# Feed-forward weights through a rounded DRAM copy and SP's queue, with new tables of order, in a four-layer transformer kernel

## The chip, the cores and the metric

The kernel runs on one NeuronCore of a Trainium2 chip. The metric is the device time of one execution in microseconds; 3622.65 is the median of three runs of the kernel before (3621.72 to 3628.54).

The engines go by short names: PE is TensorE, DVE is VectorE, ACT is ScalarE, POOL is GpSimd, SP is SyncE, which issues transfers and computes nothing. Every engine carries out its own instructions in a written order and waits on semaphores for the others.

## The reference

The input x is 8 batches of 512 tokens of width 256, in fp32. Four residual layers follow one another, each behind a layer norm:

```python
x = x + attn_a(layernorm(x)); x = x + ffn(layernorm(x))
x = x + attn_b(layernorm(x)); x = x + ffn(layernorm(x))     # the same ffn weights both times

# attn_a: 16 heads of 64; the "sequence" of the softmax is the 64 components of one head of one token
scores[q, k] = Q[q] * K[k] / 8, masked to k <= q;  w = softmax_k(scores);  out[q] = sum_k w[q, k] * V[k]
# attn_b: ordinary causal attention over the 512 tokens, 16 heads of 16
# ffn: ternary weights (-1, 0, 1) with scales by row
h = silu(x @ w1.T * s1) * (x @ w2.T * s2)
h = gelu(h @ h1.T * s_h1);  h = gelu(h @ h2.T * s_h2);  out = h @ w3.T * s3
```

So attn_a is elementwise work: for each token and head a triangle of 64 x 64 products, exponentials and weighted sums. It falls to POOL, DVE and ACT. The feed-forward layers and attn_b fall mostly to PE.

## The kernel before

**Attention A.** A unit of work is one block of 128 tokens (i of 4) and one group of four heads (g of 4): 16 units for each batch, 128 in all. The lower triangles of a unit are cut into squares of width n = 32, 16, 8, 4, 2 and 1, kept in four tiles: unit 0 and unit 2 of `units` (32-wide squares), unit 1 (16-wide), and unit 3 (8, 4, 2 and 1). A tile goes through these steps:

- `scores` multiplies queries by keys (POOL for units 0 to 2, DVE for unit 3; L855),
- `exps` is the exponential on ACT (L878),
- `weigh` multiplies by the values on DVE (L890),
- `halve` adds one half of a 128 x 4096 tile to the other by an accumulating 1 MB transfer that POOL issues (L897),
- for unit 2, `fold` adds two halves on POOL (L905),
- the sums over the columns follow: unit 0 by 16 accumulating transposes on PE (`sums32`, L918), a copy, a turn back and an add on DVE (L1000); the others by DVE reduces (`gather`, L1047) and adds on POOL (`adds`, L1063).

DVE then inverts the denominators (`invert`, L1069), POOL multiplies (`divide`, L1075), PE turns the group over and projects it out (L1085, L1101, L535).

**The order.** A unit has a period of 12 slots. The table `G["order"]` gives every step a slot relative to the unit's start and, by its place in the table, a rank within the slot; `first` is the table of batch 0. Units overlap, since the slots run from -120 to 36. A manual schedule keeps the written order on PE, DVE, ACT and POOL.

**The rest.** A generator (`after_a`) yields the feed-forward layer, attn_b and the second feed-forward layer of each batch piece by piece. The main loop interleaves it with attention A of the following batch: `G["pace"]` prices the pieces, and `G["total"]` is what is spent on them over the 16 units of a batch. Attention A of batch 0 runs alone at the start, and the rest of the last batch alone at the end.

**Feed-forward weights.** PE multiplies them in a rounded type, F32R, while DRAM holds fp32. A pass reads 11 tiles of 128 x 2048 (1 MB): two for the gates (L1293), eight hidden ones (L1365) and w3 (L1398). There are two passes for each batch, so 16 passes and 176 loads. The pool `hwp` has three buffers. `Weights.ahead` issues the load after the next one; POOL issues it, as a transfer that converts on the way. The weights of attn_b (`wbqk`, `wbvp`) come in the same sequence from SP. In the last pass `fits` loads the unrounded tiles once more by SP (L1250) and compares them with the rounded ones on DVE.

SP also issues attention A's weights (L730, L732, L738), x and the stores of the output.

Of the kernel before, what the change touches and what calls it, by code (L numbers as in the profile page):

```python
# [16 lines left out]
P = 128  # L17
# [28 lines left out]
 'half': [0, 0, 0, 0, 1, 1],  # L46
 'order': [[8, 'scores', 2, 1, 2], [10, 'exps', 2], [22, 'small_squares'], [20, 'add16'], [-120, 'load'],
           [-26, 'normalise'], [6, 'exps', 1], [13, 'sums32', 0], [23, 'adds', 3], [32, 'turn_group'],
           [22, 'keep_sums', 2], [16, 'keep16'], [9, 'weigh', 1], [-1, 'scores', 0, 0, 2], [11, 'fold', 0],
           [12, 'turn16'], [6, 'halve', 0], [11, 'scores', 3, 0, 1], [-30, 'ahead'], [14, 'sums16'],  # L50
           [22, 'add32', 2], [12, 'weigh', 2], [21, 'turn_sums', 2], [34, 'project_out'],
           [4, 'scores', 1, 1, 2], [-8, 'project'], [10, 'halve', 1], [36, 'new_x'], [25, 'divide'],
           [13, 'weigh', 3], [7, 'scores', 2, 0, 2], [15, 'turn_sums', 0], [17, 'fold', 2], [32, 'keep_att'],
           [-5, 'keep_qk'], [12, 'halve', 2], [13, 'keep_sums', 0], [18, 'add32', 0], [18, 'gather', 3],
           [-22, 'turn_x'], [24, 'invert'], [13, 'gather', 1], [16, 'adds', 1], [20, 'sums32', 2],
           [12, 'exps', 3], [4, 'weigh', 0], [3, 'exps', 0], [1, 'scores', 1, 0, 2], [-22, 'keep_x'],
           [0, 'scores', 0, 1, 2]],
 'first': {'sum': ['pe16', 'pe16'],
           'p16': 2,
           'sum16': 'dve',  # L60
           'order': [[21, 'small_squares'], [23, 'adds', 3], [21, 'sums32', 2], [-23, 'turn_x'],
                     [29, 'divide'], [0, 'scores', 0, 1, 2], [4, 'scores', 1, 0, 2], [15, 'turn16'],
                     [26, 'invert'], [19, 'add32', 0], [6, 'scores', 2, 0, 2], [6, 'halve', 0],
                     [-1, 'scores', 0, 0, 2], [-27, 'normalise'], [9, 'fold', 0], [7, 'exps', 1],
                     [10, 'exps', 2], [20, 'gather', 3], [15, 'turn_sums', 0], [4, 'weigh', 0],
                     [23, 'turn_sums', 2], [15, 'weigh', 3], [-120, 'load'], [-30, 'ahead'], [16, 'keep16'],
                     [10, 'scores', 3, 0, 1], [-21, 'keep_x'], [17, 'adds', 1], [19, 'sums16'],
                     [23, 'add32', 2], [8, 'weigh', 1], [10, 'halve', 1], [36, 'new_x'],
                     [4, 'scores', 1, 1, 2], [13, 'weigh', 2], [-5, 'keep_qk'], [6, 'scores', 2, 1, 2],
                     [14, 'exps', 3], [31, 'turn_group'], [21, 'add16'], [21, 'keep_sums', 2],  # L70
                     [15, 'gather', 1], [32, 'keep_att'], [13, 'fold', 2], [14, 'sums32', 0],
                     [14, 'keep_sums', 0], [-8, 'project'], [34, 'project_out'], [13, 'halve', 2],
                     [2, 'exps', 0]],
           'on': ['adds0']},
 'sum16': 'dve',
 'lo': 'psum',
 'pace': {'gate': 1.8, 'attn': 0.65, 'wait': 1.354, 'w3': 1.05, 'out': 0.95, 'turn': 0.997},
 'total': 304.842,
 'eps': 'dve',
# [7 lines left out]
       'attn': 72,  # L87
       'proj': 21}}

# [243 lines left out]
def fast_path(ctx: ExitStack, tc: tile.TileContext, k, t, flag):  # L333
# [216 lines left out]
    def bank_half(j):  # L550
        return bank[:, j, :]
# [86 lines left out]
    JB = 8  # L638

    def kind(b, n_u):  # L640
        c = G["first"] if b == 0 and "first" in G else G
        return c["sum"][n_u // 2] if n_u in (0, 2) else c.get("sum16", "dve")

    def reds(b):
        return (G["first"] if b == 0 and "first" in G else G).get("red", [])

    def on(b):
        return (G["first"] if b == 0 and "first" in G else G).get("on", [])

    def p16(b):  # L650
        return (G["first"] if b == 0 and "first" in G else G)["p16"]

# [3 lines left out]
    def pieces(w, n, off, nsq, cols, b, n_u, parts):  # L656
# [6 lines left out]

        if n < 16:
            e, ev = (
# [42 lines left out]
    class AttentionA:  # L708
# [32 lines left out]
        def slot(self, t):  # L741

            now = []
            for lo, hi, order in TABLES:
                for place, (slot, what, args) in enumerate(order):
                    late = 8 if what in ("normalise", "turn_x", "keep_x") and t - slot in (12, 20) else 0
                    n, r = divmod(t - slot - late, 12)
                    if r == 0 and lo <= n < hi and (late == 0 or t - slot == 20):
                        now.append((place / len(order), what, self.todo[n] + args))
            for _, what, args in sorted(now, key=lambda p: p[0]):  # L750
                getattr(self, what)(*args)
# [177 lines left out]
        def sums16(self, b, i, g):  # L929

            if kind(b, 1) == "dve": return
            assert (b, i, g, 1, "h") in self.seen
            w = self.live.pop((b, i, g, 1)).rearrange("p (j r) -> p j r", r=2 * P)
            self.take(1, 0, 1)
            for r in range(2):
                for j in range(8):
                    nc.tensor.matmul(
                        bank_half(1)[:, r * P : (r + 1) * P], w[:, j, r * P : (r + 1) * P], ident,
                        start=(j == 0 and r == 0), stop=(j == 7), is_transpose=True, skip_group_check=True,
                    )  # L940
            assert "fwd" not in self.live
            self.live["fwd"] = (b, i, g, 1)

        def keep16(self, b, i, g):

            if kind(b, 1) == "dve": return
            assert self.live.pop("fwd") == (b, i, g, 1)
            self.live["sums16"] = ap_.tile([P, 2 * P], F32, tag="red128", name="sums16", bufs=3)
            nc.scalar.copy(self.live["sums16"], bank_half(1))
            self.free(1, 0, 1)  # L950

        def turn16(self, b, i, g):

            if kind(b, 1) == "dve": return
            assert "back" not in self.live
            self.live["back"] = (b, i, g, 1)
            s16 = self.live.pop("sums16")
            self.take(1, 0, 1)
            for r in range(2):
                nc.tensor.transpose(bank_half(1)[:, r * P : (r + 1) * P], s16[:, r * P : (r + 1) * P], ident)  # L960

        def add16(self, b, i, g):

            if kind(b, 1) == "dve": return
# [3 lines left out]
            nc.vector.tensor_tensor(  # L968
                rows, rows, bank_half(1).rearrange("p (a x i) -> p a x i", a=2, i=16), ALU.add
            )  # L970
            assert (b, i, g, 0, "w") in self.seen
            self.free(1, 0, 1)
            self.done[b, i, g] += 1
# [40 lines left out]
        def small_squares(self, b, i, g):  # L1014
# [4 lines left out]
            for n, off, nsq, cols in squares(units[NU - 1]):  # L1019
                if n <= 2 and n not in reds(b):  # L1020
# [3 lines left out]
                    self.add_rows(b, i, g, n, cols, both[..., 0], "small")  # L1024
            if (b, i, g, NU - 1, "r") in self.seen: self.live.pop((b, i, g, NU - 1))

        def gather(self, b, i, g, n_u):
# [4 lines left out]
            w = self.live[b, i, g, n_u]  # L1032
            if n_u < NU - 1 or (b, i, g, n_u, "s") in self.seen: self.live.pop((b, i, g, n_u))
            self.sums[b, i, g, n_u] = []
            here = 0
            for n, off, nsq, cols in sorted(squares(units[n_u]), key=lambda u: u[0] in reds(b)):
                if n in reds(b):
                    assert all((b, i, g, k, what) in self.seen for k in range(NU) for what in "pew")
# [87 lines left out]
    def flush():  # L1126
        fns = pending[:]
        pending.clear()
        for fn in fns:
            fn()  # L1130

    class Weights:

# [3 lines left out]
        def __init__(self):  # L1137
            def ffn():
                for i in range(MC // 4):
                    yield "gate", F32R, nc.gpsimd, t.w12p[i]  # L1140
                for layer in range(2):
                    for i in range(MC // 2):
                        yield "hidden", F32R, nc.gpsimd, t.h12[layer, i]
                yield "w3", F32R, nc.gpsimd, t.w3p

            def all_of_them():
                for b in range(NB):
                    yield from ffn()
                    yield "wbqk", F32, nc.sync, wbqk_d
                    yield "wbvp", F32, nc.sync, wbvp_d  # L1150
                    yield from ffn()

            self.n, self.todo, self.loaded = 0, all_of_them(), []
            for _ in range(2):
                self.ahead()

        def ahead(self):
            what = next(self.todo, None)
            if what is not None:
                name, dtype, eng, src = what  # L1160
                w = hwp.tile([P, HB], dtype, tag="hw", name=f"{name}_{self.n}")[:, : src.shape[-1]]
                eng.dma_start(w, src)
                self.loaded.append(w)
                self.n += 1
# [594 lines left out]
```

## Time and profile before

| What | Value |
|---|---|
| median of three runs | 3622.65 us |
| profiled execution, its own time | 3620.43 us |
| its span | 3618.6 us |
| mean granted clock of PE | 0.916 |
| busy, share of the span | PE 84%, DVE 86%, ACT 69%, POOL 82% |
| software queue (POOL's transfers) | 587.24 MB, 71.1% of 16 DMA engines |
| hardware queue (SP's and ACT's transfers) | 75.02 MB, 6.0% |
| halvings, issue to landing | 384 of 1 MB, median 7.6 us |
| feed-forward weights, issue to landing | 128 + 32 + 16 of 1 MB, median 6.0 to 6.7 us |

A row of a group of instructions reads: line, engine, operation, output<-input, shapes, count | busy us, mean ns of one | idle us of the engine just before them, and what ended that idle time. "L1162" is the line of `ahead` that issues a weight load. In the timeline the first two columns are the start and the duration in us. The chain of waits follows the work that ended last back to the beginning, and "w<-w" as a transfer is a halving. A duration can overlap that of the instruction behind it on the same engine.

### The profile page before, as it was taken

The page shows a single profiled execution, that of the slowest core. Times are in us where ns is not written, and L with a number is a line of the kernel's source. Part 1 is how long each engine was busy: PE and PEld are TensorE (multiplying, and loading weights), DVE is VectorE, ACT ScalarE, POOL GpSimd, SP SyncE. Part 2 cuts the span into 40 slices and gives each one's busy share as a digit, 9 for nine tenths or more (in the row PEclk, how much of TensorE's full clock was granted, in tenths as well). Part 3 has the DMA queues.
Part 4 walks back from the last instruction along what each step waited for, and adds up shares of the span by engine and source line. Part 5 has one row for each costly group of instructions (what it writes and reads, how often), then busy time and mean ns, then how long its engine had stood idle before and what let it go on. Part 6 is the DMA issues. An engine that isn't in the chain of part 4 may idle for free.

```text
span 3618.6 us, 42449 instructions
## 1 busy us (share of the span) xinstructions
PE 3048.9 (84%) x14468; PEld 2168.6 (60%) x14468; DVE 3124.0 (86%) x3844; ACT 2505.2 (69%) x3488; POOL 2971.8 (82%) x2682
## 2 busy tenths in 40 slices
PE   7765698798887998888987988879888889878998
PEld 4544475476645766466754766457664667556756
DVE  7999998999889998999988998899989998896227
ACT  4544686687767787687866877668866878665453
POOL 7999988888898989989898888989889888885000
PEclk8878799898998999998998989989999999989999
DMA  9978897688877988689876888769877788767414
GB/s 240 200 160 165 178 228 163 149 215 194 206 165 167 231 206 185 141 204 213 224 167 144 217 191 204 167 155 232 195 190 150 193 208 209 175 146 221 131 53 170
DMA packets 117038, 665.34 MB, mean 184 GB/s; under 512 B 12742, under 2 KB 30665, under 8 KB 43467
## 3 DMA queue, kind: packets, MB, share of 16 engines
q0 software_dynamic: 80640, 587.24, 71.1%
q1 hardware_dynamic: 35896, 75.02, 6.0%
q8 instruction: 116, 1.90, 0.2%
q14 instruction: 110, 0.90, 0.1%
q10 hardware_dynamic: 276, 0.27, 0.0%
HBM read 251.18 MB, written 8.65 MB: 72 GB/s over the span
## 4 chain that ended last, share of the span: by engine, by line
PE 33%; DVE 22%; POOL 17%; ACT 14%; issue 9%; DMA 5%; ACTq 0%; POOLq 0%; SPq 0%; DVEq 0%
POOL w L855 8%; PE ph L1365 8%; DVE w L890 6%; DVE red L1047 5%; DMA w<-w 5%; PE pw L1293 4%; POOL acc L1063 3%; PE pyb L1523 3%; ACT w L878 3%; DVE ws L855 3%; PE pqkb L1444 3%; PE bank L918 3%; PE psb L1511 2%; POOL w L897 2%; PE qv L808 2%
## 5 line engine op out<-in xcount | busy, mean ns | idle before, releaser
L855 POOL TENSOR_TENSOR w<-k 128x1024 f32<-128x1024 f32 x768 | 1617.6, 2194 | 44.2 <-DVE red L1047 23.0
L1365 PE MATMUL ph<-h,hidden 128*128 128x512 f32 x4096 | 1019.6, 403 | 6.5 <-DVE h L1277 2.4
L890 DVE TENSOR_TENSOR w<-w,qv 128x1024 f32<-128x1024 f32 (+1 forms) x624 | 890.2, 1458 | 83.9 <-ACT w L878 83.8
L1365 PEld LDWEIGHTS ph<-h,hidden 128*128 128x128 f32 x4096 | 766.4, 190 | 186.7 <-issue 21.0
L878 ACT ACTIVATE w<-w 128x2048 f32<-128x2048 f32 x384 | 734.6, 1915 | 138.5 <-POOL w L855 136.5
L897 POOL DMA_DIRECT2D w<-w x384 | 352.3, 918 | 193.3 <-DVE w L890 94.7
L1293 PE MATMUL pw<-xnt,gate 128*128 128x512 f32 (+2 forms) x1152 | 346.4, 452 | 153.4 <-ACT silu L1268 99.3
L1047 DVE TENSOR_REDUCE red<-w 128x256 f32<-128x2048 f32 x240 | 426.8, 1778 | 23.7 <-DMA w<-w 22.0
L1047 DVE TENSOR_REDUCE red<-ws 128x256 f32<-128x2048 f32 (+1 forms) x256 | 435.6, 1742 | 0.0
L1063 POOL TENSOR_TENSOR acc<-acc,red 128x256 f32<-128x256 f32 x496 | 392.1, 791 | 29.5 <-DVE red L1047 11.0
L1293 PEld LDWEIGHTS pw<-xnt,gate 128*128 128x128 f32 x1152 | 236.3, 225 | 242.1 <-ACT silu L1268 124.0
L918 PE MATMUL bank<-ident,w 128*128 128x128 f32 x2304 | 322.6, 301 | 52.1 <-ACT x L1114 26.4
L855 DVE TENSOR_TENSOR ws<-qv,k 128x1024 f32<-128x1024 f32 (+3 forms) x512 | 300.0, 647 | 76.9 <-POOL acc L1063 76.8
L918 PEld LDWEIGHTS bank<-ident,w 128*128 128x128 f32 x2304 | 298.3, 158 | 80.0 <-ACT x L1114 39.2
L890 DVE TENSOR_TENSOR ws<-ws,qv 128x1024 f32<-128x1024 f32 (+3 forms) x512 | 294.9, 636 | 32.0 <-ACT ws L878 32.0
L905 POOL TENSOR_TENSOR w<-w 128x1024 f32<-128x1024 f32 x112 | 280.2, 2502 | 50.7 <-DMA w<-w 50.6
L808 PE MATMUL qv<-wqv,xnta 128*128 128x512 f32 x512 | 269.9, 653 | 27.3 <-DVE ws L890 22.0
L878 ACT ACTIVATE ws<-ws 128x1920 f32<-128x1920 f32 x128 | 233.1, 1821 | 76.2 <-DVE ws L855 72.6
L1331 DVE TENSOR_TENSOR h<-ph,h 128x512 fp32r<-128x512 f32 x256 | 167.8, 681 | 90.3 <-ACT ph L1327 84.1
L1518 ACT ACTIVATE eb<-psb 128x512 f32<-128x512 f32 (+3 forms) x503 | 181.9, 459 | 89.2 <-PE psb L1515 88.9
L1326 ACT ACTIVATE h<-ph,s_sb 128x512 fp32r<-128x512 f32 x256 | 176.6, 690 | 94.2 <-PE ph L1365 92.2
L1069 DVE RECIPROCAL acc<-acc 128x256 f32<-128x256 f32 x128 | 223.1, 1743 | 3.9 <-POOL acc L1063 3.9
(163 smaller groups left out, 4867.5 us busy)
## 6 DMA issues: line engine op xcount, KB each, us to landing
w<-w POOLq DMA_DIRECT2D x384, 1024.0 KB, 7.6
hidden<-in_h POOLq DMA_DIRECT2D x128, 1024.0 KB, 6.4
gate<-in_w12p POOLq DMA_DIRECT2D x32, 1024.0 KB, 6.7
w<-in_w3p POOLq DMA_DIRECT2D x16, 1024.0 KB, 6.0
wqv<-wqv_d SPq DMA_DIRECT2D x31, 512.0 KB, 3.9
wo<-in_wo SPq DMA_DIRECT2D x32, 256.0 KB, 7.4
w<-in_h SPq DMA_DIRECT2D x8, 1024.0 KB, 6.9
wk<-wk_d SPq DMA_DIRECT2D x31, 256.0 KB, 6.2
```

The source lines that it names most:

```text
L808: nc.tensor.matmul(qv.rearrange("p j f -> p (j f)"), xnt[:, c, :], wqv[:, c, :], start=(c == 0), stop=(c == DC - 1),)
L855: eng.tensor_tensor(e, rows(q).to_broadcast(shape), columns(kt[:, 0]).to_broadcast(shape), ALU.mult)
L878: nc.scalar.activation(e, e, AF.Exp, scale=C**-0.5)
L890: nc.vector.tensor_tensor(ev, e, columns(qv[:, 1]).to_broadcast(list(e.shape)), ALU.mult)
L897: nc.gpsimd.dma_start(w[:, :2048], w[:, 2048:], accum_op=ALU.add)
L905: nc.gpsimd.tensor_tensor(w[:, :1024], w[:, :1024], w[:, 1024:2048], ALU.add)
L918: nc.tensor.matmul(bank_half(G["half"][4])[:, :P], w[:, j * P : (j + 1) * P], ident, start=(j == 0), stop=(j == n - 1), is_transpose=True,)
L1047: nc.vector.tensor_reduce(red, self.columns_of(w, n, off, nsq), AX.X, ALU.add)
L1063: (nc.vector if what == "psum" or what in on(b) else nc.gpsimd).tensor_tensor(rows, rows, part.rearrange("p a (x i) -> p a x i", i=n), ALU ...
L1069: nc.vector.reciprocal(acc[:, 0, :], acc[:, 0, :])
L1293: nc.tensor.matmul(pj[:, toks], w[:, m % 4, j, c, :], xs[:, p, c, toks], start=(p == 0 and c == 0), stop=(p == 1 and c == DC - 1),)
L1365: nc.tensor.matmul(pss[j], w[:, j, c, :], h_in(p, c), start=(p == 0 and c == 0), stop=(p == 1 and c == MC - 1),)
```

## The change

**Weights.** A DRAM tensor `rounded` of eleven tiles is added. In the first pass a tile is loaded by POOL as before, and SP then stores the rounded tile. In the other 15 passes SP loads it from there, without conversion.

```diff
+    rounded = dram.tile([MC // 4 + MC + 1, P, HB], F32, name="rounded")
...
         def ahead(self):
             what = next(self.todo, None)
             if what is not None:
-                name, dtype, eng, src = what
+                name, dtype, k, src = what
                 w = hwp.tile([P, HB], dtype, tag="hw", name=f"{name}_{self.n}")[:, : src.shape[-1]]
-                eng.dma_start(w, src)
+                if k is None or k in self.kept:
+                    nc.sync.dma_start(*((w, src) if k is None else (w.bitcast(F32), rounded[k])))
+                else:
+                    nc.gpsimd.dma_start(w, src)
+                    nc.sync.dma_start(rounded[k], w.bitcast(F32))
+                    self.kept.add(k)
```

**Kinds of units.** A unit now has a place (0 to 15) in its batch, and `G["kinds"]` may change how it is done. In batches 1 to 7 the units at places 13 and 14 get `sum8: pe`: their 8-wide squares are laid out by columns and summed by PE in place of a DVE reduce and a POOL add. Batch 0 keeps its own settings.

```diff
+ 'kinds': {'3': {}, '4': {}, '13': {'sum8': 'pe'}, '14': {'sum8': 'pe'}, '0': {}}}
...
+        def sums8(self, b, i, g):
...
+            for r in range(2):
+                for j in range(8):
+                    nc.tensor.matmul(
+                        bank_half(h)[:, r * P : (r + 1) * P], w[:, r * SMALL + j * P : r * SMALL + (j + 1) * P], ident,
+                        start=(j == 0 and r == 0), stop=(j == 7), is_transpose=True, skip_group_check=True,
+                    )
...
+        def keep8(self, b, i, g):
...
+            nc.scalar.copy(self.live["sums8"], bank_half(h))
...
+        def turn8(self, b, i, g):
...
+            for r in range(2):
+                nc.tensor.transpose(bank_half(h)[:, r * P : (r + 1) * P], s8[:, r * P : (r + 1) * P], ident)
...
+        def add8(self, b, i, g):
...
+            nc.vector.tensor_tensor(
+                rows, rows, bank_half(h).rearrange("p (a x i) -> p a x i", a=2, i=8), ALU.add
+            )
```

**The layout.** Both tables are written anew. The steps of the 16-wide sums on PE, which no unit used, go out and those of the 8-wide sums come in. In the main table most steps keep their slot or move by one; these move by more, or change their place on an engine:

| Step | slot before | slot after | on its engine |
|---|---|---|---|
| `scores` 1, second part | 4 | 1 | POOL, still behind the first part |
| `divide` | 25 | 27 | POOL, now behind `scores` 1 and `adds` 1 |
| `sums32` 2 (a reduce) | 20 | 21 | DVE, now behind `weigh` 1 |
| `halve` 1 | 10 | 10 | POOL, now ahead of `add32` 2 |
| `halve` 0 | 6 | 7 | POOL, the same place |
| `exps` 1 | 6 | 5 | ACT, the same place |

```diff
- 'pace': {'gate': 1.8, 'attn': 0.65, 'wait': 1.354, 'w3': 1.05, 'out': 0.95, 'turn': 0.997},
- 'total': 304.842,
+ 'pace': {'gate': 1.8, 'attn': 0.65, 'wait': 1.422, 'w3': 1.05, 'out': 0.76, 'turn': 0.997},
+ 'total': 304.757,
```

## The prediction

> **What bounds the kernel now.** I read the page first (busy time, chain), then the busy time by stage, because the mean over the span mixes three stages with different limits.
>
> ```profile
> PE 3048.9 (84%) x14468; PEld 2168.6 (60%) x14468; DVE 3124.0 (86%) x3844; ACT 2505.2 (69%) x3488; POOL 2971.8 (82%) x2682
> ...
> PE 33%; DVE 22%; POOL 17%; ACT 14%; issue 9%; DMA 5%; ACTq 0%; POOLq 0%; SPq 0%; DVEq 0%
> ```
>
> No engine is full and no engine holds half of the chain. The stages (us of busy time in each window; last three columns are granted clock, DMA share, GB/s):
>
> ```profile
> 120.00:400.00 280.00, 176.31 (x770) 123.33 (x767) 272.17 (x290) 140.23 (x164) 262.39 (x219) 0.79 0.81 170
> 460.00:3300.00 2840.00, 2446.99 (x11787) 1742.95 (x11786) 2569.76 (x3176) 2126.90 (x2934) 2519.45 (x2253) 0.93 0.80 188
> 3300.00:3618.00 318.00, 293.88 (x1470) 221.32 (x1468) 135.42 (x199) 136.81 (x262) 38.48 (x69) 0.96 0.43 141
> ```
>
> First attention alone: DVE is busy for 97% and sets the time; no weights are loaded there. Last, feed-forward alone: PE 92%, POOL 12%; a cheaper POOL is worth nothing. Between them lie 2840 us with DVE 90%, POOL 89%, PE 86%: three engines near full, each following a written order, so one late step stops the others in turn. The change lives there. POOL's rows and waits in that stage:
>
> ```profile
> L897 POOL DMA_DIRECT2D w<-w x321 | 293.4, 914 | 177.7 <-DVE w L890 87.2 <-ACT ws L878 36.7 <-issue 15.5
> L905 POOL TENSOR_TENSOR w<-w 128x1024 f32<-128x1024 f32 x107 | 267.8, 2503 | 47.0 <-DMA w<-w 46.9
> L1162 POOL DMA_DIRECT2D hidden<-in_h x107 | 89.6, 837 | 0.0
> L1162 POOL DMA_DIRECT2D gate<-in_w12p x26 | 20.0, 769 | 6.2 <-PE bank L1085 5.1 <-PE ph L1365 1.2
> L1162 POOL DMA_DIRECT2D w<-in_w3p x13 | 10.5, 810 | 0.0
> ```
>
> There are 146 weight loads on POOL, which hardly ever wait (6.2 us): the buffer is free before POOL arrives. They cost their own duration. POOL's longer idle times lie before the halvings (L897), where it waits for DVE's weighing, and before the fold (L905), where it waits for a halving to land. The timeline of POOL shows one load's price and place:
>
> ```profile
> 1758.53 0.87 POOL L897 DMA_DIRECT2D w<-w  x1
> 1759.13 0.84 POOL L1162 DMA_DIRECT2D hidden<-in_h  x1
> 1759.70 1.85 POOL L1063 TENSOR_TENSOR acc<-acc,red 128x256 f32<-128x256 f32 x2
> 1761.51 1.99 POOL L855 TENSOR_TENSOR w<-k 128x1024 f32<-128x1024 f32 x1
> 1763.86 0.87 POOL L897 DMA_DIRECT2D w<-w  x1 [0.36 <-issue]
> ...
> 1776.19 2.40 POOL L905 TENSOR_TENSOR w<-w 128x1024 f32<-128x1024 f32 x1 [3.75 <-DMA w<-w]
> ```
>
> The load's record is 0.84 us, but the next instruction starts 0.57 us after it; the median over the 146 is 0.61 us. The halving issued at 1763.86 stands in the same queue behind that load and lands only about 12 us later (the chain has it as a 12.24 us piece); POOL's fold then waits 3.75 us.
>
> **1. POOL loses the issues.** Of 176 loads 165 leave, eleven (the first pass) stay. In the middle stage about 139 leave: 139 x 0.61 = 85 us of POOL's order. What of it is on the path: the chain of waits, read through that stage, holds 48 pieces of L1162 past the first pass, 26 us in sum. A piece on the chain is saved only until the next late engine, one off it may become worth something, so the bounds are 0 and -85. I take **-26 us**. In the tail, loads on POOL wait up to 16 us, but POOL is idle there: 0.
>
> **2. SP gains the loads.** SP is idle but for DMAs, and issues cost it 0.33 us. It will arrive early and stand waiting for PE to release the buffer. Queued behind: wqv, wk, wo, wbqk, wbvp, x and the output stores. wqv and wk wait for a PE product that is written later than the one the weight load waits for, so their wait ends last anyway, and a unit of about 26 us passes before they are used: 0.
>
> **3. The transfers.** Does a plain load from SP move faster than a converting one? In the tail, issue to landing:
>
> ```profile
> hidden<-in_h POOLq DMA_DIRECT2D x16, 1024.0 KB, 5.3
> w<-in_h SPq DMA_DIRECT2D x6, 1024.0 KB, 5.9
> ```
>
> No gain; the trace's packet records agree (8 KB packets: 325 ns converting, 309 to 324 from SP, about 640 for a halving, eight per engine and transfer: 2.6, 2.5, 5.1 us). So the DMA engines stay 80% busy, and only who waits for whom changes. Now a load delays the halvings behind it in its queue; the halvings land in 7.3 us (median) where no weights are loaded and in 7.7 us, at worst 13.6, in the middle stage. From another queue a load can take engine time from a halving already running, and can no longer make one behind it wait in line. Today 43 of 321 halvings (13%) are waited for (27 by the fold, 13 by DVE's reduce, 3 by PE), so 139 x 2.6 x 13% = 47 us bounds it in either direction; I take **0**.
>
> The Trainium skill, page "DMA: Bandwidth & Descriptors", section "Issuing engines are not separate DMA queues", says that transfers from all issuers interleave on the same 16 engines and that another issuer saves just the issue time, usually small beside the DMA. That speaks against any gain beyond item 1, and item 3's rows agree for bandwidth. The same page, "Queues, rings and completion order", says that each DMA engine takes the queues in turn, packet by packet; by that a halving in flight always pays for a load, and the sum would take the upper end of item 3 and come out near 3638. The middle stage's 7.3 to 7.7 us shows only one queue's behaviour, so no row here decides it.
>
> **4. Eleven stores of 1 MB into the DRAM store**, in the first feed-forward pass. 11 x 2.6 = 29 us of engine time; with the same 13%, +4 (0 to +29). Each holds SP until its load has landed (5 to 7 us), and its buffer a little longer; three buffers cover that. **+4 us**.
>
> **5. The 8-wide sums of two units per batch go to PE** (places 13 and 14, batches 1 to 7: 14 units). DVE gives up a reduce of 2.28 us (128x2048) and takes an add of about 0.41 (the row L834, 128x256 with a PSUM operand): 14 x 1.87 = 26 us; at DVE's 22% of the chain -6. POOL gives up one add of 0.89: 12 us, at 17% -2. PE takes 16 products (1.76 us as chain pieces of 16 at L918) and two turns (0.44): 31 us, at 33% +10. ACT takes a copy of 0.37: 5 us, +1. **+3 us**, bounds -38 and +36.
>
> **6. The order.** Set out by slot modulo 12, each engine's order is nearly the old one. What differs: DVE does the 16-wide weighing before the reduce of the third unit of squares (1.21 us), not after; POOL issues that halving before, not after, a 0.46 us add; POOL's divide comes after two score products instead of before them (4.4 us later; it is followed by the turn of the group, six slots later, some 13 us, which covers it). In the middle stage 13 of POOL's 44 waits for the weighing, 35.6 us, stand before this halving. Each can shrink by up to 1.67: 0 to -22, I take **-10**. The feed-forward pacing moves from "out" to "wait", the total stays (304.842 to 304.757): 0. The first batch's order is changed as little, where DVE is full: 0.
>
> **Sum:** -26 + 0 + 0 + 4 + 3 - 10 = -29. Against the profiled execution, 3620.4 us (span 3618.6 and 1.8 around it), that is **3591 us**. That execution is 2 us under the median of the three runs, 3622.65. A measurement of this kernel can tell 0.2%, 7 us, from no change.
>
> **Rivals.**
> - *POOL sets the pace* (0.18). With POOL at 89% and DVE waiting 64 us for POOL's adds, all 85 us of item 1 and 22 of item 6 could come through: 3513; with half of it, 3567. For it: two of the three full engines are relieved. Against it: POOL has just 17% of the chain, and waits 178 us before halvings already; DVE's 90% leaves little.
> - *The freed time becomes waits* (0.08). POOL reaches the halvings sooner and waits longer for DVE's weighing and ACT's exponentials; the row of 87.2 grows by what L1162 lost. 3615 to 3630.
> - *The loads slow the halvings* (0.22, slower). Place: 1 MB halvings in flight, waited for by L905 and L1047. At today's 13% it is +47, total 3638; at 20% (+72) 3663. It decides against the change once these waits grow from 67 us (46.9 + 13.4 + 6.8) past 96, or the median landing passes 8.8 us (7.7 plus 139 x 2.6 / 321).
> - *PE is late in the units with PE sums* (0.06, slower): item 5 at +36 and half of item 1, 3637.
> - The change not doing what it says would show as more than eleven L1162 rows on POOL; SP's row for w<-in_h is already a plain 1 MB load, so I give this no chance of its own.
>
> **How the numbers follow.** The forecast has 0.46, 3575 to 3610 by itself. Faster by over 0.2%: 0.46 + 0.18 = 0.64; within it 0.08; slower 0.22 + 0.06 = 0.28. The range runs from 3530 (into the first rival, its far end left out) to 3645 (takes in the slower rivals at today's share, leaves out the 20% case); about 0.17 is left out.
>
> **What would show it.** L1162 on POOL falls from 176 rows to eleven, and SP has 165. Right: POOL's busy time down by about 85 us in the middle stage, median landing of the halvings at or below 8 us, L905's wait for DMA near 47 us, period of a batch (422 us between the same unit's divides) down by 3 to 5 us. Wrong: POOL's idle time before L897 grown by as much as L1162 gave up; halvings above 8.8 us; SP's loads landing so late that PE waits for "hidden" (now 1.9 us); PE's units after places 13 and 14 longer than 26 us with ACT waiting for its sums.

## The result: 1.6% slower

The changed kernel takes 3685.43 us (median of four runs, 3676.08 to 3690.22) against 3623.28 for the kernel before: a ratio of 1.0164, 95% interval 1.0143 to 1.0184. The forecast was 3591, its range 3530 to 3645. The profiled execution took 3682.82 us with a span of 3681.0.

The changed kernel's page, busy time and chain:

```profile
PE 3075.3 (84%) x14720; PEld 2192.7 (60%) x14720; DVE 3102.9 (84%) x3844; ACT 2497.2 (68%) x3492; POOL 2863.3 (78%) x2503
...
PE 35%; DVE 21%; POOL 15%; ACT 12%; DMA 11%; issue 6%; POOLq 0%; ACTq 0%; SPq 0%; DVEq 0%
DMA w<-w 11%; PE ph L1437 11%; POOL w L871 7%; DVE w L906 6%; DVE red L1113 5%; PE pyb L1595 4%; POOL acc L1129 3%; PE pw L1365 3%; ACT w L894 3%; PE pqkb L1516 2%; PE psb L1583 2%; PE bank L934 2%; DVE ws L871 2%; DVE ws L906 2%; PE qv L824 2%
```

POOL is 109 us less busy, as it should be, but the share of transfers in the chain of waits went from 5% to 11%, and all of that is halvings (w<-w). Its groups of instructions in the window 460 to 3300 us (the lines moved: 913 is the halving, 921 the fold, 1232 the load in `ahead`):

```profile
L913 POOL DMA_DIRECT2D w<-w x315 | 280.3, 890 | 199.1 <-DVE w L906 97.0 <-ACT ws L894 48.8 <-issue 14.3
L921 POOL TENSOR_TENSOR w<-w 128x1024 f32<-128x1024 f32 x106 | 257.7, 2431 | 113.4 <-DMA w<-w 109.0 <-DVE mv L595 2.8 <-DVE rstd L594 1.5
L1232 POOL DMA_DIRECT2D hidden<-in_h x6 | 4.4, 726 | 0.0
```

The loads are gone from POOL but for the first pass. In their stead POOL's fold waits 109.0 us for halvings, where it waited 46.9. Busy time by stage:

```profile
120.00:400.00 280.00, 177.53 (x766) 130.43 (x764) 270.28 (x287) 138.31 (x162) 259.71 (x217) 0.79 0.80 169
460.00:3360.00 2900.00, 2472.78 (x12028) 1759.43 (x12027) 2553.37 (x3181) 2121.16 (x2940) 2431.69 (x2103) 0.93 0.79 187
3360.00:3681.00 321.00, 298.58 (x1506) 225.32 (x1504) 138.10 (x202) 141.54 (x269) 24.55 (x43) 0.97 0.41 141
```

The middle window is drawn 60 us longer than before; DVE's busy time in it has not grown (2569.76 before), granted clock (0.93) and DMA share are as they were. Transfers, from issue to landing:

```profile
w<-w POOLq DMA_DIRECT2D x384, 1024.0 KB, 8.0
hidden<-rounded SPq DMA_DIRECT2D x120, 1024.0 KB, 7.7
gate<-rounded SPq DMA_DIRECT2D x30, 1024.0 KB, 10.9
```

The halvings' median moved by 0.4 us only, from 7.6. So the median is not where the loss shows.

Where the 62 us of span went, by the starts of POOL's divides (the last step of a unit on POOL) in the timelines: the 17th divide, end of batch 0's units, at 394.2 before and 400.4 after: +6.2. The batch with the first feed-forward pass, 422.8 to 441.4: +18.6. The 95 units behind it: +37.3. The tail: +0.3.

### The profile page after: what moved, and what is told of

Same layout as the page of the kernel before. It is cut to its first block, busy times and chain, and to the rows that moved or that the text cites. A ratio compares the mean times of both kernels' runs of the same rounds, so it can differ in the third digit from the quotient of the medians.

```text
span 3681.0 us, 43032 instructions
## 1 busy us (share of the span) xinstructions
PE 3075.3 (84%) x14720; PEld 2192.7 (60%) x14720; DVE 3102.9 (84%) x3844; ACT 2497.2 (68%) x3492; POOL 2863.3 (78%) x2503
## 4 chain that ended last, share of the span: by engine, by line
PE 35%; DVE 21%; POOL 15%; ACT 12%; DMA 11%; issue 6%; POOLq 0%; ACTq 0%; SPq 0%; DVEq 0%
DMA w<-w 11%; PE ph L1437 11%; POOL w L871 7%; DVE w L906 6%; DVE red L1113 5%; PE pyb L1595 4%; POOL acc L1129 3%; PE pw L1365 3%; ACT w L894 3%; PE pqkb L1516 2%; PE psb L1583 2%; PE bank L934 2%; DVE ws L871 2%; DVE ws L906 2%; PE qv L824 2%
## 5 line engine op out<-in xcount | busy, mean ns | idle before, releaser
L871 POOL TENSOR_TENSOR w<-k 128x1024 f32<-128x1024 f32 x768 | 1571.1, 2174 | 60.9 <-PE bank L934 54.2
L913 POOL DMA_DIRECT2D w<-w x384 | 342.1, 891 | 227.8 <-DVE w L906 106.3
L1365 PE MATMUL pw<-xnt,gate 128*128 128x512 f32 (+2 forms) x1152 | 331.7, 438 | 144.8 <-ACT silu L1340 112.1
L1129 POOL TENSOR_TENSOR acc<-acc,red 128x256 f32<-128x256 f32 (+1 forms) x482 | 372.4, 773 | 63.7 <-DVE red L1113 45.6
L1113 DVE TENSOR_REDUCE red<-ws 128x256 f32<-128x2048 f32 (+1 forms) x242 | 405.1, 1712 | 0.0
L934 PE MATMUL bank<-ident,w 128*128 128x128 f32 x2304 | 330.7, 305 | 65.3 <-ACT x L1180 36.3
L921 POOL TENSOR_TENSOR w<-w 128x1024 f32<-128x1024 f32 x112 | 272.8, 2435 | 123.6 <-DMA w<-w 114.8
L1365 PEld LDWEIGHTS pw<-xnt,gate 128*128 128x128 f32 x1152 | 224.9, 216 | 230.3 <-ACT silu L1340 142.5
```

The costliest lines, as they stand in the source:

```text
L871: eng.tensor_tensor(e, rows(q).to_broadcast(shape), columns(kt[:, 0]).to_broadcast(shape), ALU.mult)
L913: nc.gpsimd.dma_start(w[:, :2048], w[:, 2048:], accum_op=ALU.add)
L921: nc.gpsimd.tensor_tensor(w[:, :1024], w[:, :1024], w[:, 1024:2048], ALU.add)
L934: nc.tensor.matmul(bank_half(G["half"][4])[:, :P], w[:, j * P : (j + 1) * P], ident, start=(j == 0), stop=(j == n - 1), is_transpose=True,)
L1113: nc.vector.tensor_reduce(red, self.columns_of(w, n, off, nsq), AX.X, ALU.add)
L1129: (nc.vector if what == "psum" or what in on(b) else nc.gpsimd).tensor_tensor(rows, rows, part.rearrange("p a (x i) -> p a x i", i=n), ALU ...
```

## Experiments

Each group shared the runs of the kernel before on its chip (medians 3620.6 to 3625.7 us over the groups); ratios are against them. Theory C in the expectations is contention of the two queues, rival L the new layout. "Old tables" are those of the kernel before. The cuts of code show the main lines of each edit.

### Weights and layout apart

**New tables, loads by POOL.** The changed kernel with

```diff
-                if k is None or k in self.kept:
...
+                (nc.sync if k is None else nc.gpsimd).dma_start(w, src)
```

> The new tables, pace and PE sums, but all 176 weight loads converting on POOL as before, no DRAM store. Theory C (contention: loads from SP's queue take DMA time from halvings in flight): the layout alone is not to blame, 3600 to 3640 us, halvings near 7.7 us, POOL's fold waiting for DMA near 47 us in the middle stage. Rival L (the new tables are the loss): 3670 to 3710, with DVE's and POOL's waits of the changed kernel.

Measured: 3684.81, ratio 1.0172 (1.0143 to 1.0201). The new tables lose as much without SP's loads as the whole change does.

**Old tables, loads by SP.** The kernel before with `rounded` and the new `Weights`, nothing else.

> The old tables, pace and sums; only the weights change: eleven converting loads, eleven stores, 165 loads by SP. Theory C: 3660 to 3700 us, fold's wait for DMA over 90 us. Rival L: POOL has lost its issues and nothing else moved, 3580 to 3625 us, fold's wait near 47 us.

Measured: 3677.67, ratio 1.0155 (1.0124 to 1.0186). SP's loads, with the stores that they need, also lose alone. Both times that theory C and rival L named came in: each of the two changes costs some 60 us alone, and together they cost no more than either. The first run also says that taking SP's loads out of the changed kernel would not have saved it. Whether contention is the reason for the loss by SP's loads is tested below.

**Without the PE sums.**

```diff
- 'kinds': {..., '13': {'sum8': 'pe'}, '14': {'sum8': 'pe'}, '0': {}}}
+ 'kinds': {..., '13': {}, '14': {}, '0': {}}}
```

> The changed kernel without the PE sums of places 13 and 14 (their 8-wide squares go to DVE and POOL as elsewhere). Theory C and rival L alike: within 15 us of the changed kernel, 3670 to 3700. Rival S (the PE sums hold up PE and the shared PSUM bank, seen in ACT's longer wait for the turn of the group): 3650 or less.

Measured: 3688.17, ratio 1.0186 (1.0157 to 1.0215), the changed kernel's time. Rival S falls.

**New tables, POOL loads plain from the store.**

```diff
-                    nc.sync.dma_start(*((w, src) if k is None else (w.bitcast(F32), rounded[k])))
+                    if k is None:
+                        nc.sync.dma_start(w, src)
+                    else:
+                        nc.gpsimd.dma_start(w.bitcast(F32), rounded[k])
```

> The changed kernel, but the 165 later loads are issued by POOL from the DRAM store (plain, no conversion), so that they stand in one queue with the halvings again and POOL pays for the issues. Theory C: the same as the first run of this group within 10 us (3600 to 3640): the queue matters, the conversion does not. Rival L: 3680 to 3720, the issues of POOL coming on top.

Measured: 3709.50, ratio 1.0237 (1.0206 to 1.0268): 25 us over converting loads, in rival L's range. The batch with the stores took 442.2 us between divides instead of 424.4; the five batches behind it 436.2 and 435.6 on average. So the stores cost 18 us there, and dropping the conversion is worth nothing that shows.

### What the loads are worth, and which queue they stand in

**Old tables, no loads.** One tile takes the place of all eleven, and `hwp`, which then holds only attn_b's weights, has two buffers instead of three:

```diff
+    fixed = const.tile([P, HB], F32R, name="fixed")
+    nc.gpsimd.dma_start(fixed, t.h12[0, 0])
...
+                if k is not None:
+                    self.loaded.append(fixed)
+                    self.n += 1
+                    return
```

> The old tables with the feed-forward loads left out altogether: one tile of weights, loaded once, stands in for all eleven in every pass (so the products are not the reference's), and there are no stores. POOL issues no load and no load competes with a halving. Theory C (SP's loads take time from halvings in flight): 3535 to 3600 us, fold's wait for DMA under 40 us. Rival P (the old order is fitted to its own durations, POOL's loads among them, and loses by any shift): 3640 or more, with the waits for DMA small.

Measured: 3580.73, ratio 0.9884 (0.9868 to 0.9901). Theory C's marks are met and rival P falls: the old order bears a shift. All issues and all bytes of the loads together are worth 41 us. POOL's rows of this kernel in the window 460 to 3300:

```profile
L897 POOL DMA_DIRECT2D w<-w x324 | 296.1, 914 | 260.5 <-DVE w L890 162.6 <-ACT ws L878 35.0 <-DVE acc L1000 14.6
L905 POOL TENSOR_TENSOR w<-w 128x1024 f32<-128x1024 f32 x109 | 274.5, 2518 | 15.8 <-DMA w<-w 15.4
```

The wait for DVE's weighing grew from 87.2 to 162.6 us: most of POOL's 85 us became that wait.

**New tables, no loads**, by the same edit in the changed kernel.

> The new tables in the same way, without feed-forward loads and stores. Theory C with the new tables as a separate loss of some 60 us: 60 us above the run before it in this group. If the new tables lose only where transfers are late: within 15 us of that run.

Measured: 3617.62, ratio 0.9991 (0.9981 to 1.0002): 37 us above the run before it, between the 60 and the 15 that were expected, with the fold waiting 2.7 us in all. The tables lose that much with no weight load to blame and hardly a wait for a halving. Of their 64 us some 27 go with the loads.

**Old tables, POOL loads plain**, the edit of the fourth run in the second.

> The old tables with stores, and the 165 later loads plain from the DRAM store but issued by POOL, in one queue with the halvings. Against the old tables with SP's loads (3678) only the issuer differs. Theory C: 3635 to 3645 (the time before and the 18 us that the batch with the stores has lost). Rival (reading from the new DRAM tensor, or something else in the weights' path, costs the time): 3670 to 3690.

Measured: 3633.35, ratio 1.0036 (1.0021 to 1.0051), just under theory C's range and far from the rival's. POOL's fold in this kernel, then in the second run, same window:

```profile
L905 POOL TENSOR_TENSOR w<-w 128x1024 f32<-128x1024 f32 x107 | 266.0, 2486 | 49.9 <-DMA w<-w 49.7
```

```profile
L905 POOL TENSOR_TENSOR w<-w 128x1024 f32<-128x1024 f32 x105 | 255.4, 2432 | 137.4 <-DMA w<-w 133.7 <-DVE mv L595 3.6
```

Same bytes, same stores, same tables: 44 us and 84 us of fold waits hang on who issues the load.

### Queue or time of issue

**SP's loads held to POOL's place**, in the second run's kernel:

```diff
+                    if k is not None:
+                        nc.gpsimd.memset(w.bitcast(F32)[:, :1], 0.0)
                     nc.sync.dma_start(...)
```

> The old tables with SP's loads and the stores, but each of the 165 loads is held back to the place where POOL used to issue it: POOL clears one column of the buffer there, and SP's transfer waits for that. Only the queue still differs from the run with plain loads by POOL (3633). Theory Q (a load in a second queue takes DMA time from a halving in flight): 3660 to 3680, fold's wait for DMA above 100 us. Rival T (SP starts the load too early, as soon as PE frees the buffer): 3620 to 3640, fold's wait near 45 us.

Measured: 3622.57, ratio 0.9999 (0.9983 to 1.0014). The fold in this kernel:

```profile
L905 POOL TENSOR_TENSOR w<-w 128x1024 f32<-128x1024 f32 x107 | 262.1, 2450 | 56.7 <-DMA w<-w 56.5
```

Theory Q, 3660 to 3680 with over 100 us of this wait, falls. In SP's queue, but no earlier than POOL would have issued them, the loads do no harm; from the 33rd divide to the last this kernel is 13.6 us faster than before, and the stores take that back (14.7 us in their batch). What hurts is an early issue. (No run holds SP's loads under the new tables.) The place can be seen in the second run, SP's and then POOL's timeline:

```profile
1643.64 0.32 SPq L1164 DMA_DIRECT2D hidden<-rounded  x1
```

```profile
1639.72 0.88 POOL L897 DMA_DIRECT2D w<-w  x1
...
1645.26 0.88 POOL L897 DMA_DIRECT2D w<-w  x1 [1.11 <-ACT ws L878]
...
1657.47 2.37 POOL L905 TENSOR_TENSOR w<-w 128x1024 f32<-128x1024 f32 x1 [4.12 <-DMA w<-w]
```

SP's load slips in between the halving of the 16-wide squares (1639.72) and the one of unit 2 (1645.26), which the fold waits for. That halving lands some 12 us after its issue, and the fold stands for 4.12 us. I paired every fold from 700 to 3300 us with the loads issued around its halving, from the timelines of POOL and SP (the last two rows are runs of the next group):

| Kernel | units with a load issued in that window | fold waits there, us | other units | fold waits there, us |
|---|---|---|---|---|
| before | 8 | 25.6 | 90 | 16.1 |
| changed | 40 | 68.3 | 57 | 29.5 |
| old tables, SP | 36 | 97.5 | 61 | 26.0 |
| old tables, SP held | 8 | 20.8 | 91 | 25.0 |
| before, none in the window | 0 | 0 | 98 | 12.4 |
| before, many in the window | 42 | 128.8 | 54 | 7.1 |

In the units with a load in the window the fold waits 1.7 to 3.2 us on average, in the others 0.1 to 0.5, whoever issues the load. POOL, which issues in order, is seldom there. SP mostly waits for PE to free the buffer and starts then (its longest wait in the second run, us in total, times, longest), and it is there in four units of ten:

```profile
SPq L1164 <- PE ph L1371: 833.5, 90, 13.4
```

The fold is not alone: in the second run (old tables, SP) DVE's reduce waits 48.5 us for halvings, where it waited 13.4.

### The window put to the test

**Loads kept out of the window**, kernel before, POOL converting:

```diff
             nc.gpsimd.dma_start(w[:, :2048], w[:, 2048:], accum_op=ALU.add)
+            held["last"] = n_u
+            if n_u == 2:
+                issue_held()
...
-                eng.dma_start(w, src)
+                    issue = lambda: nc.gpsimd.dma_start(w, src)
+                    if held["last"] == 1:
+                        held["loads"].append(issue)
+                    else:
+                        issue_held()
+                        issue()
```

> The kernel before, converting loads on POOL as they were, but loads that fell between these two halvings are issued behind the second one. Theory W: fold's wait for DMA falls from 42 us to some 20 in the middle stage, 3600 to 3615. Rival: no change, 3615 to 3630.

**Loads put into it**: the same with loads held while the last halving is that of unit 0, until that of unit 1 is issued.

```diff
-            if n_u == 2:
+            if n_u == 1:
...
-                    if held["last"] == 1:
+                    if held["last"] == 0:
```

> The opposite: the kernel before, converting loads on POOL, but loads whose place falls behind the halving of the first unit of squares are put off until the 16-wide halving is issued, and so stand just ahead of the halving that the fold waits for. One queue, no SP, no stores. Theory W: fold's wait for DMA grows to 80 us or more, 3640 to 3680. Rival (the place in the order is harmless while all stand in one queue): 3615 to 3630.

Measured: 3607.27, ratio 0.9962 (0.9949 to 0.9974), and 3710.09, ratio 1.0244 (1.0231 to 1.0257). The folds of the first and of the second, window 460 to 3300:

```profile
L915 POOL TENSOR_TENSOR w<-w 128x1024 f32<-128x1024 f32 x107 | 269.6, 2519 | 12.6 <-DMA w<-w 12.5
```

```profile
L915 POOL TENSOR_TENSOR w<-w 128x1024 f32<-128x1024 f32 x104 | 255.4, 2455 | 147.1 <-DMA w<-w 146.9
```

One queue, no SP, no stores, the same instructions: moving the issue by a few instructions spans 103 us. The first of the two is the version that beats both kernels. Theory W holds, and the second loses more than the 3640 to 3680 expected. Not all of that need be the fold's: with the loads put into the window, PE waits for weights that came late, 28.3 us against 1.9 in the kernel before, and the mean granted clock of the profiled execution was 0.905 against 0.916.

```profile
PE ph L1385 <- DMA hidden<-in_h: 28.3, 10, 5.5
```

**Held loads, store filled in the first stage**: SP loads a tile, ACT rounds it, SP stores it, at two steps a tile behind `bound_scores`.

```diff
+            fine = block(f"fine_{k}", F32R)
+            nc.scalar.copy(fine, raws[k])
+            yield
+            nc.sync.dma_start(rounded[k], fine.bitcast(F32))
```

> Old tables, SP's loads held to POOL's place, and the DRAM store filled earlier: in the first stage SP loads each tile as it is, ACT rounds it by a copy into a free block, SP stores it. No converting load is left and the first pass reads the store too. If the stores beside the first pass cost their 12 to 18 us there and the holding gives 11 to 14 us per run (3622 against 3633 with POOL's plain loads): 3598 to 3612. If ACT's copies or the early transfers delay the first stage by as much: 3615 to 3630.

Measured: 3639.27, ratio 1.0044 (1.0029 to 1.0058), a miss: the 17th divide moved from 394.2 to 423.9 us, 30 us for eleven loads, eleven copies on ACT and eleven stores in a stage whose DMA share rose from 0.81 to 0.92. The stores' cost was moved and nearly doubled. Transfers and copies were not tried apart.

**The same, kept out of the window.**

> The same, and a load whose place falls between the issue of the 16-wide halving and that of the halving that POOL's fold waits for is put behind the latter. Theory W (a load issued in that window costs the fold about 2.7 us; the held run had eight such units with 20.8 us of waits): 10 to 20 us below the run before it, fold's wait under 30 us. Rival (the waits move to the loads put off or to PE): within 5 us of it.

Measured: 3634.45, ratio 1.0031 (1.0020 to 1.0042): 5 us better, at the edge of the rival; theory W's 10 to 20 us and its mark of under 30 us for the fold were missed. The fold still waits 42 us; 32.1 of the 40.5 between 700 and 3300 stand in units whose load now comes behind the halving (20 of these 54 wait). In POOL's own queue the fold waits 7.0 us in 62 such units. That fits a second queue taking time from a halving in flight: some 0.6 us a unit, the smaller part.

### What of the new layout loses

**The divide back**: the changed kernel with

```diff
- 'order': [[1, 'scores', 1, 0, 2], ...
+ 'order': [[25, 'divide'], [1, 'scores', 1, 0, 2], ...
-            ... [27, 'divide'], ...
```

> The changed kernel with POOL's divide back at slot 25 ahead of the 16-wide score products. Theory D (the late divide makes PE's turn of the group late, and ACT, waiting 142 us to copy it, is what the new tables lose): 3625 to 3660. Rival (the place of the divide is covered, as the prediction said): 3675 to 3695, ACT's wait for the turn unchanged.

Measured: 3689.95, ratio 1.0183 (1.0166 to 1.0200), in the rival's range. Theory D falls.

**One part of the layout each**, all else as in the kernel before (in short form): the new main table; the new pace and total; the new table of batch 0.

```diff
+ 'order': (the changed kernel's)                                  # first run
+ 'pace': {..., 'wait': 1.422, ..., 'out': 0.76, ...}, 'total': 304.757,   # second run
+ 'first': (the changed kernel's)                                  # third run
```

> The kernel before (converting loads by POOL, no store, no PE sums, old first table, pace and total) with the new main table alone. If the main table carries the loss of the new layout: 3655 to 3690. If pace and first table carry it: 3615 to 3640.

> The kernel before with the new pace and total alone (wait 1.422, out 0.76). If the pace matters little: 3615 to 3630. If it carries a part of the loss by shifting the feed-forward pieces against the units: 3635 to 3670.

> The kernel before with the new table of batch 0 alone. The runs with both new tables reached the 17th divide 6 to 9 us later, so 3625 to 3635; 3615 to 3624 if the table of batch 0 costs nothing by itself.

Measured: 3662.46, ratio 1.0113 (1.0093 to 1.0132); 3659.21, ratio 1.0094 (1.0076 to 1.0112); 3629.50, ratio 1.0008 (0.9997 to 1.0018). Main table and pace cost some 37 and 34 us, the table of batch 0 nothing that can be told. The pace, two numbers that leave the total nearly alone, was put at zero. With the main table the longest wait of ACT, then the same of the kernel before (us in total, times, longest):

```profile
ACT att L1232 <- PE bank L1228: 122.6, 59, 5.2
```

```profile
ACT att L1089 <- PE bank L1085: 62.8, 69, 3.0
```

**That step moved**: the main table's run with the turn back at 32, and the kernel before with it at 33.

```diff
-[33, 'turn_group'], ... [33, 'keep_att']
+[32, 'turn_group'], ... [32, 'keep_att']
```

> The run with the new main table alone (3662), with PE's turn of the group and ACT's copy of it back from slot 33 to 32. Theory K (one slot later, PE has another feed-forward piece ahead of the turn, and ACT, next in its order, stands for it: 123 us of waits against 63): 3625 to 3645, ACT's wait for the turn near 65 us. Rival (the loss is spread over the table): 3650 to 3670.

> The kernel before with these two steps alone moved from slot 32 to 33. Theory K: 3640 to 3665 and ACT's wait for the turn above 110 us. Rival: 3615 to 3632.

Measured: 3651.99, ratio 1.0082 (1.0063 to 1.0101), and 3618.64, ratio 0.9983 (0.9970 to 0.9996). In the second, ACT's wait rose to 100.2 us and the kernel got no slower. The conspicuous wait is not the loss; theory K falls but for some 10 us in the new table. Another wait grew by about as much as the loss: DVE's reduce of the 16-wide squares, for their halving, with the main table and then before:

```profile
DVE red L1190 <- DMA w<-w: 61.6, 22, 6.1
```

```profile
DVE red L1047 <- DMA w<-w: 13.4, 13, 2.2
```

With the turn moved back it is still 57.1 us, with the new pace 20.0. In 18 of the 22 waits a load was issued between the first unit's halving and this one, in 10 of 13 before. So it looks like the same collision at another halving, 48 us of waits beside a loss of 37; no run puts it to the test, and what the pace costs its time by stays open.

## Why the prediction was wrong, step by step

- **Item 3 (transfers, taken as 0) failed.** It gave a bound of 47 us either way and no reason why gain and loss should cancel; between SP's and POOL's plain loads lay 44 us of loss. That the bound has this size is luck: it was reckoned with 13% of the halvings waited for, and in the changed kernel it was 74 of 315, 23%. The rival "the loads slow the halvings" named place and waits rightly: 46.9 + 13.4 + 6.8 us became 109.0 + 40.1 + 9.9, past its mark of 96. Its reason was only half right. It spoke of halvings in flight; holding SP's loads took all of the loss back, so the cost is the time of issue, and the runs in one queue show it at the halving that the fold waits for. Its second mark, a median landing of 8.8 us, was not reached (8.1 in the stage): 40 units in a hundred with a load ahead of one of their three halvings hardly move a median. The row that held the answer was shown: the load of 1759.13 stood ahead of the halving issued at 1763.86, and the fold waited 3.75 us. I read it as a price of the load's being in the same queue, and did not ask how often a load would stand there when SP issues it.
- **Item 2 (SP gains the loads, 0) failed with it.** "SP will arrive early" was right. What an early issue collides with was looked for only in SP's own queue.
- **Item 1 (-26) was right in kind.** Held loads gave 11 us over POOL's plain loads, with a marker of 0.3 us left on POOL for each. Without any loads 41 us came back, so my -85 was no real bound: POOL's wait for the weighing took up the rest, as the rival "the freed time becomes waits" had it.
- **Item 4 (stores, +4) was mis-sized**, though within its 0 to +29: 18 us in their batch, 12 over the run. In the run with POOL's plain loads, between 394 and 840 us, the waits for halvings rose from 6.4 to 14.9 us at the fold, from 1.2 to 17.8 at DVE's reduce and from none to 6.4 at PE.
- **Item 5 (+3) held** as far as these runs can tell: without the PE sums the time is the same. DVE's add took 0.41 us, as costed.
- **Item 6 (-10, bounds 0 and -22) failed.** Main table +37, pace +34. I compared each engine's order of attention steps and found it nearly the same, but never the place of those steps against the feed-forward pieces and their loads, which slots and pace set, and excluded a loss without a reason. I hoped for a gain ahead of the 16-wide halving; behind it DVE's reduce waited 61.6 us instead of 13.4. That this wait is the main table's loss, and the shifted pieces the pace's, is argued and not shown. The divide, the one step I worried over, is indeed covered.
- That the two losses, 57 and 64 us alone, make 62 together no step foresaw, and no run explains it. The traces give a hint: the fold waits 133.7 us for halvings with SP's loads alone and 109.0 in the changed kernel, DVE's reduce 61.6 with the new tables alone and 40.1 there.

## What to carry to other kernels

Here the cost of loads moved to an idle queue was set by when they were now issued. Before such a move, list which transfers will stand behind the load, and which of those is waited for at once. An engine that is late can be a useful gate; a tiny dependent write keeps it when the issue moves. Count such collisions unit by unit, since a median over all transfers hid them here.

## What the runs showed of the hardware

- With a 1 MB load issued just ahead of a 1 MB halving, the fold behind it waited 1.7 to 3.2 us on average, from POOL's one queue (25.6 us in 8 units, 128.8 in 42) as from SP's beside it (97.5 in 36, 68.3 in 40).
- Converting on the way cost nothing that shows: 3622 us with POOL's converting loads, 3633 with its plain ones, and the batch in which the stores are written accounts for the difference (440.3 against 422.8 us between divides).
- Eleven 1 MB loads and eleven 1 MB stores from SP, with eleven copies of 1.9 us on ACT between them, cost 30 us in the attention-only stage, with the DMA share there going from 0.81 to 0.92.
